# A gated recurrence on one core: GpSimd's wait moved to half A's hh transpose, the x transpose in quarters, and five memsets on VectorE

## The chip, the cores and the metric

The kernel runs on one core of a Trainium2 chip. The metric is the device time of one execution in microseconds; where several runs are shown it is their median. The engines are called PE (TensorE's matmuls; PEld is its weight load), DVE (VectorE), ACT (ScalarE), POOL (GpSimd) and SP (SyncE, which issues the DMAs).

## The reference, cut to what matters

For a batch of 8, 512 time steps and 512 features, a recurrence runs over the steps, and its states are added to the input. In the kernel's shorthand r is the first half of the fused gates, z the second, and hh is `h @ wh_W + wh_b`.

```python
def step(h, x_t):
    fused = sigmoid(concatenate([x_t, h], -1) @ w_W + w_b)
    hidden_state, output_state = split(fused, 2, -1)       # r, z
    memory_state = x_t @ wx_W + wx_b + hidden_state * (h @ wh_W + wh_b)
    h_new = output_state * h + (1.0 - output_state) * tanh(memory_state)
    return h_new, h_new
_, hs = scan(step, h0, swapaxes(x, 0, 1))
return x + swapaxes(hs, 0, 1)
```

All is float32.

## The kernel before, in words

**Tiling.** The 512 units of the state lie as 128 partitions by 4 chunks. Chunks 0 and 1 are half A, chunks 2 and 3 half B. For each half the state is kept in a ring of eight buffers (hT, lines 97 to 101; NH = 8). A buffer has 32 columns, of which the 8 of the batch for this step's place s in its group of four steps are filled, and the others stay zero. So a matmul whose stationary operand is such a buffer adds to the 8 rows of its own step only. Four steps (GS = 4) make a group g, and s is the place in it.

**PSUM.** There are two sets of banks, one for each parity of the group: A holds hh, z and r of half A (192 columns), Z holds z of half B (64), B holds r and hh of half B (128). Two further banks, xp, gather x times its weights for a whole group: `prefill` (line 154) issues sixteen matmuls of 384 columns a group, four in each step. `seed` (line 150, ScalarE) puts the bias into xp first, `spread` (line 166, ScalarE) copies the gates' parts from xp into the next group's banks A, B and Z, and `turn_x` (line 171, VectorE) transposes the 128 columns X, which are x @ wx_W, into the tile md1.

**The step.** The loop at line 194 is unrolled 512 times, under a schedule written out by hand, so every engine gets its instructions in the order of the text. PE runs ORDER (line 20): A0 B0 A1 with half A's new state as weights, A2 A3 with half B's, then the rest of B, then Z, then four xp matmuls of the group after the next. VectorE's order is in lines 284 to 295. Per half there are three transposes of PSUM (r and z by `turned` at L223, hh by `turn_h` at L235), the scan `memory` (L252: hh times r plus x), the product `kept` (L263: z times h) and the scan `update` (L275: the new state into the ring). ScalarE (act, L145) does the sigmoids of r, z and minus z, and tanh. After the two halves come, by s, spread A (s = 0), spread B and Z (s = 1), turn_x of the next group (s = 2), or seed of the group g + 3 (s = 3), which writes the bank that turn_x of the next group has read. Last, GpSimd adds state and input into the output tile (L308), one instruction a half. Every 16 steps SP loads 256 KB of x and stores 256 KB of output.

**The wait for GpSimd.** `update` of step i overwrites the ring buffer that GpSimd read seven steps earlier. The wait for that is not put on update but on `kept`, ahead of it on VectorE, and only once there is such an addition, from i = 8 on:

```python
inst = nc.vector.tensor_tensor(
    hd1[hf][i % 2][:, :, :, 1], ...
).ins
if i + 1 - NH in pool_done:
    tc.add_manual_dep(inst, pool_done[i + 1 - NH][hf].name, SYNC)
```

An instruction that waits for two semaphores has a wait instruction ahead of it (EVENT_SEMAPHORE in the trace, on the same line). Such instructions lie on the queue of the engine, but don't count as busy.

Of the kernel before, what the change touches and what calls it, by code (L numbers as in the profile page):

```python
# [13 lines left out]
NQ = 4  # L14
GS = 4
B = 8
HU = 64
SYNC = mybir.DependencyInfo(mybir.DependencyClass.Sync, mybir.DependencyReason.DATA)

ORDER = "A0 B0 A1 A2 A3 B1 B2 B3 Z0 Z1 Z2 Z3"  # L20
# [3 lines left out]
XP = {"A": slice(0, 192), "Z": slice(192, 256), "X": slice(256, 384), "B": slice(384, 512)}  # L24
# [3 lines left out]
def tile_cond_rnn_residual(  # L28
# [31 lines left out]
    nc = tc.nc  # L60
# [12 lines left out]
    def load_x(c):  # L73
        if c < NCH:
            t_ = xin_p.tile([P, NQ, TC * B], F32, tag="xin", name=f"xin_{c}")
            nc.sync.dma_start(out=t_, in_=x[c].rearrange("p (k n) -> p k n", k=NQ))
            xins[c] = t_
# [14 lines left out]
    for k in range(NQ):  # L92
# [4 lines left out]
    NH = 2 * GS  # L97
    hT = [
        [const.tile([P, 32, 2, 2], F32, name=f"hT{n}{i}") for i in range(NH)]
        for n in "AB"  # L100
    ]

    md0 = [[const.tile([P, 32, 2, 2], F32, name=f"md0{n}{i}") for i in range(2)] for n in "AB"]
    md1 = [const.tile([P, 2, 32, 2, 2], F32, name=f"md1{i}") for i in range(2)]
    hd0 = [[const.tile([P, B, 2, 2], F32, name=f"hd0{n}{i}") for i in range(2)] for n in "AB"]
    hd1 = [[const.tile([P, B, 2, 2], F32, name=f"hd1{n}{i}") for i in range(2)] for n in "AB"]
    zs = [[const.tile([P, 2, B], F32, name=f"z{n}{i}") for i in range(2)] for n in "AB"]
    zeros = const.tile([P, 32], F32, name="zeros")
    for t_ in [zeros] + hT[0] + hT[1] + hd0[0] + hd0[1] + md0[0] + md0[1]:
        nc.gpsimd.memset(t_, 0.0)  # L110

    def state(hf, i):

        s = i % GS
        return hT[hf][i % NH][:, B * s : B * s + B, :, 1]
# [12 lines left out]
    xps = [psum.tile([P, 512], F32, name=f"xp{q}") for q in range(2)]  # L128

    def mm(out_, lhsT, rhs, start=False):  # L130
        nc.tensor.matmul(  # L131
            out_, lhsT, rhs, start=start, stop=False, skip_group_check=True
        )
# [10 lines left out]
    def act(key, *args, **kw):  # L144
        inst = nc.scalar.activation(*args, **kw).ins  # L145
        if key in written:
            tc.declare_no_dep(inst, written[key], reason="ordered through VectorE")
        written[key] = inst

    def seed(g):  # L150

        nc.scalar.copy(xps[g % 2], bias)

    def prefill(g):

        c, t0 = divmod(g * GS, TC)
        for k in range(NQ):
            for j in range(NQ):
                mm(
                    xps[g % 2][32 * j : 32 * j + 32, 64:448],  # L160
                    xins[c][:, k, t0 * B : t0 * B + 32],
                    wx[:, k, j, :],
                )
            yield

    def spread(g, names):

        for n in names:
            nc.scalar.copy(banks[g % 2][n], xps[g % 2][:, XP[n]])

    def turn_x(g):
        nc.vector.transpose(
            md1[g % 2][:, :, :, :, 1].rearrange("p h n c -> p h c n"), xps[g % 2][:, XP["X"]]
        )

    def take(it, n=None):
        while n is None or n > 0:
            if next(it, it) is it:
                return
            n = None if n is None else n - 1  # L180
# [3 lines left out]
    for g in range(2):  # L184
        seed(g)
        take(prefill(g))
        if g == 0:
            spread(0, "ABZ")
            turn_x(0)
            seed(0)  # L190
    ctx.enter_context(tc.manual_schedule())

    pool_done = {}
    for i in range(T):
        g, s = divmod(i, GS)
        c, t = divmod(i, TC)
        ps = banks[g % 2]
        if t == 0:
            load_x(c + 3)
            ot = out_p.tile([P, NQ, TC, B], F32, tag="ot", name=f"ot_{c}")  # L200
        if s == 0:
            pre = prefill(g + 2) if g + 2 < NG else iter(())

        for n in ORDER.split():
            bank, k = n[0], int(n[1])
            hs = hT[k // 2][i % NH][:, :, k % 2, 1]
            for j in range(NQ):
                mm(ps[bank][32 * j : 32 * j + 32, :], hs, wh[:, k, j, WH[bank]])
        take(pre, 1)

        rows = slice(B * s, B * s + B)
        def flat(t_):
            return t_.rearrange("p n c s -> p (n c s)")

        raw = {
            "h": (ps["A"][:, :HU], ps["B"][:, HU:]),
            "z": (ps["A"][:, HU : 2 * HU], ps["Z"]),
            "r": (ps["A"][:, 2 * HU :], ps["B"][:, :HU]),
        }

        def turned(n, hf):
            t_ = work.tile([P, 2, 32], F32, tag=f"t{n}{hf}", name=f"t{n}{hf}_{i}")
            nc.vector.transpose(t_.rearrange("p c n -> p (c n)"), raw[n][hf])  # L223
            return t_[:, :, rows]

        def turn_r(hf):
            act(
                ("r", hf, g % 2, s),
                md0[hf][g % 2][:, rows, :, 1].rearrange("p n c -> p c n"),
                turned("r", hf),  # L230
                AF.Sigmoid,
            )

        def turn_h(hf):
            nc.vector.transpose(  # L235
                md1[g % 2][:, hf, :, :, 0].rearrange("p n c -> p c n"), raw["h"][hf]
            )

        def turn_z(hf):
            tz = turned("z", hf)  # L240
            act(("z", hf, i % 2), zs[hf][i % 2], tz, AF.Sigmoid)
            act(
                ("zc", hf, i % 2),
                hd0[hf][i % 2][:, :, :, 1].rearrange("p n c -> p c n"),
                tz,
                AF.Sigmoid,
                scale=-1.0,
            )

        def memory(hf):  # L250
            m = work.tile([P, B, 2, 2], F32, tag=f"m{hf}", name=f"m{hf}_{i}")
            nc.vector.tensor_tensor_scan(  # L252
                flat(m),
                flat(md0[hf][g % 2][:, rows]),
                flat(md1[g % 2][:, hf, rows]),
                0.0,
                ALU.mult,
                ALU.add,
            )
            act(("n", hf, i % 2), hd1[hf][i % 2][:, :, :, 0], m[:, :, :, 1], AF.Tanh)  # L260

        def kept(hf):
            inst = nc.vector.tensor_tensor(  # L263
                hd1[hf][i % 2][:, :, :, 1],
                zs[hf][i % 2].rearrange("p c n -> p n c"),
                state(hf, i),
                ALU.mult,
            ).ins

            if i + 1 - NH in pool_done:  # L270
                tc.add_manual_dep(inst, pool_done[i + 1 - NH][hf].name, SYNC)

        def update(hf):
            s1 = (i + 1) % GS
            nc.vector.tensor_tensor_scan(  # L275
                flat(hT[hf][(i + 1) % NH][:, B * s1 : B * s1 + B]),
                flat(hd0[hf][i % 2]),
                flat(hd1[hf][i % 2]),
                0.0,
                ALU.mult,  # L280
                ALU.add,
            )

        turn_r(0)
        turn_h(0)
        turn_z(0)
        memory(0)
        turn_h(1)
        kept(0)
        turn_r(1)  # L290
        update(0)
        turn_z(1)
        memory(1)
        kept(1)
        update(1)

        if g + 1 < NG:
            if s == 0:
                spread(g + 1, "A")
            elif s == 1:  # L300
                spread(g + 1, "BZ")
            elif s == 2:
                turn_x(g + 1)
            elif s == 3 and g + 3 < NG:
                seed(g + 3)
        done = []
        for hf in range(2):
            inst = nc.gpsimd.tensor_tensor(  # L308
                ot[:, 2 * hf : 2 * hf + 2, t, :].rearrange("p c n -> p n c"),
                xins[c][:, 2 * hf : 2 * hf + 2, t * B : t * B + B].rearrange("p c n -> p n c"),  # L310
                state(hf, i + 1),
                ALU.add,
            ).ins
            done.append(inst)
        pool_done[i + 1] = done
        if t == TC - 1:
            nc.sync.dma_start(out=out[c], in_=ot.rearrange("p k t b -> p (k t b)"))
            xins.pop(c)
# [62 lines left out]
```

## Time and profile before

| what | value |
|---|---|
| time, median of 3 runs | 1774.58 us (1774.36 to 1774.95) |
| the profiled execution's own time | 1775.63 us |
| its span (first to last instruction) | 1773.9 us |
| granted TensorE clock, mean | 0.998 |
| VectorE, instructions in the trace, waits included | 8826, of which 6274 compute |
| HBM traffic | 14.96 MB read, 8.39 MB written |
| GpSimd, L308 | 125.8 us for half A's 512 additions, 124.3 us for half B's |

The profile is one execution. In the groups and timelines a row has the line of the kernel, the engine, the operation, output and inputs by their names (buffer numbers left out), the shape and a count. Timelines begin with the start and the duration in us; idle time of the engine before an instruction and what ended it stand in brackets. VectorE's rows overlap a little[...]. In the answers on waits, a row has who waited for whom, the us in total, the times, and the longest. Transfers of instructions show in the profile as DMA queues of their own: 416 packets with 6.82 MB in one, and 116 packets with 0.94 MB in another.

### The profile page before, as it was taken

The page shows a single profiled execution, that of the slowest core. Times are in us where ns is not written, and L with a number is a line of the kernel's source. Part 1 is how long each engine was busy: PE and PEld are TensorE (multiplying, and loading weights), DVE is VectorE, ACT ScalarE, POOL GpSimd, SP SyncE. Part 2 cuts the span into 40 slices and gives each one's busy share as a digit, 9 for nine tenths or more (in the row PEclk, how much of TensorE's full clock was granted, in tenths as well). Part 3 has the DMA queues.
Part 4 walks back from the last instruction along what each step waited for, and adds up shares of the span by engine and source line. Part 5 has one row for each costly group of instructions (what it writes and reads, how often), then busy time and mean ns, then how long its engine had stood idle before and what let it go on. Part 6 is the DMA issues. An engine that isn't in the chain of part 4 may idle for free.

```text
span 1773.9 us, 121405 instructions
## 1 busy us (share of the span) xinstructions
PE 1751.6 (99%) x53312; PEld 1422.4 (80%) x53312; DVE 1129.7 (64%) x6274; ACT 857.4 (48%) x4610; POOL 253.4 (14%) x1053
## 2 busy tenths in 40 slices
PE   7999999999999999999999999999999999999998
PEld 5888888888888888888888888888888888888887
DVE  2666666666666666666666666666666666666665
ACT  2444444444454444444444444444444444444444
POOL 1111111111111111111111111111111111111111
PEclk9999999999999999999999999999999999999999
DMA  4000000000000000000000000000000000000000
GB/s 174 16 4 16 16 16 16 6 15 16 17 16 16 4 16 17 16 16 5 16 16 16 16 15 5 16 16 16 17 4 16 16 16 16 4 16 11 10 10 10
DMA packets 11236, 31.11 MB, mean 18 GB/s; under 512 B 1361, under 2 KB 1361, under 8 KB 10705
## 3 DMA queue, kind: packets, MB, share of 16 engines
q1 hardware_dynamic: 10704, 23.35, 3.9%
q8 instruction: 416, 6.82, 1.6%
q14 instruction: 116, 0.94, 0.2%
HBM read 14.96 MB, written 8.39 MB: 13 GB/s over the span
## 4 chain that ended last, share of the span: by engine, by line
PE 95%; DVE 2%; DMA 1%; ACT 1%; issue 1%; SPq 0%; POOLq 0%; DVEq 0%; POOL 0%; ACTq 0%
PE A L131 40%; PE B L131 24%; PE xp L131 18%; PE Z L131 13%; DMA hin<-in_h_dram 1%; DVE tr L223 1%; DVE hTA L275 0%; ACT md0A L145 0%; DVE m L252 0%; DVE hd1A L263 0%; DMA wx<-in_wx_dram 0%; DVE hTB L275 0%; ACT zB L145 0%; DVE tz L223 0%; DVE md L235 0%
## 5 line engine op out<-in xcount | busy, mean ns | idle before, releaser
L131 PE MATMUL A<-wh,hTA 128*32 128x192 f32 x8192 | 527.1, 327 | 11.2 <-DVE hTB L120 7.4
L145 ACT ACTIVATE md0A<-tr 128x16 f32<-128x16 f32 x512 | 120.9, 236 | 723.6 <-DVE tr L223 723.6
L131 PE MATMUL A<-wh,hTB 128*32 128x192 f32 x8192 | 455.5, 340 | 2.1 <-DVE hTB L275 1.5
L131 PEld LDWEIGHTS A<-wh,hTA 128*32 128x32 f32 x8192 | 275.8, 137 | 220.7 <-DVE hTA L275 212.5
L223 DVE STREAM_TRANSPOSE tr<-A 128x64 f32<-128x64 f32 x512 | 127.9, 250 | 479.9 <-PE A L131 479.9
L131 PE MATMUL xp<-wx,xin 128*32 128x384 f32 x4096 | 425.9, 486 | 0.0
L131 PE MATMUL B<-wh,hTA 128*32 128x128 f32 x8192 | 414.8, 273 | 0.0
L131 PEld LDWEIGHTS A<-wh,hTB 128*32 128x32 f32 x8192 | 273.2, 142 | 105.3 <-DVE hTB L275 98.9
L131 PEld LDWEIGHTS B<-wh,hTA 128*32 128x32 f32 x8192 | 325.2, 136 | 10.3
L131 PE MATMUL B<-wh,hTB 128*32 128x128 f32 x8192 | 318.3, 273 | 0.0
L308 POOL TENSOR_TENSOR ot<-xin,hTA 128x16 f32<-128x16 f32 x512 | 125.8, 246 | 1127.2 <-DVE hTA L275 1038.0
L131 PEld LDWEIGHTS B<-wh,hTB 128*32 128x32 f32 x8192 | 248.3, 136 | 0.0
L131 PE MATMUL Z<-wh,hTB 128*32 128x64 f32 x8192 | 222.6, 225 | 0.0
L131 PE MATMUL Z<-wh,hTA 128*32 128x64 f32 x8192 | 217.2, 223 | 0.0
L131 PEld LDWEIGHTS Z<-wh,hTA 128*32 128x32 f32 x8192 | 200.9, 141 | 0.0
L131 PEld LDWEIGHTS Z<-wh,hTB 128*32 128x32 f32 x8192 | 182.1, 147 | 0.0
L308 POOL TENSOR_TENSOR ot<-xin,hTB 128x16 f32<-128x16 f32 x512 | 124.3, 243 | 389.6 <-DVE hTB L275 389.6
L145 ACT ACTIVATE md0B<-tr 128x16 f32<-128x16 f32 x512 | 119.2, 233 | 108.0 <-DVE tr L223 106.6
L275 DVE TENSOR_TENSOR_SCAN hTB<-hd0B,hd1B 128x32 f32<-128x32 f32 x512 | 115.1, 225 | 55.0 <-DVE hd1B L263 1.0
L235 DVE STREAM_TRANSPOSE md<-B 128x64 f32<-128x64 f32 x512 | 146.7, 286 | 0.6 <-issue 0.5
L235 DVE STREAM_TRANSPOSE md<-A 128x64 f32<-128x64 f32 x512 | 135.8, 265 | 0.0
L252 DVE TENSOR_TENSOR_SCAN m<-md0B,md 128x32 f32<-128x32 f32 x512 | 133.8, 261 | 0.5
(42 smaller groups left out, 1767.3 us busy)
## 6 DMA issues: line engine op xcount, KB each, us to landing
xin<-in_x_dram SPq DMA_DIRECT2D x32, 256.0 KB, 3.0
out_dram<-ot SPq DMA_DIRECT2D x32, 256.0 KB, 2.1
wx<-in_wx_dram SPq DMA_DIRECT2D x4, 768.0 KB, 6.6
wh<-in_wh_dram SPq DMA_DIRECT2D x4, 768.0 KB, 13.5
bias<-in_bias_dram SPq DMA_DIRECT2D x4, 64.0 KB, 2.0
hin<-in_h_dram SPq DMA_DIRECT2D x1, 16.0 KB, 15.0
```

The source lines that it names most:

```text
L131: nc.tensor.matmul(out_, lhsT, rhs, start=start, stop=False, skip_group_check=True)
L145: inst = nc.scalar.activation(*args, **kw).ins
L223: nc.vector.transpose(t_.rearrange("p c n -> p (c n)"), raw[n][hf])
L235: nc.vector.transpose(md1[g % 2][:, hf, :, :, 0].rearrange("p n c -> p c n"), raw["h"][hf])
L252: nc.vector.tensor_tensor_scan(flat(m), flat(md0[hf][g % 2][:, rows]), flat(md1[g % 2][:, hf, rows]), 0.0, ALU.mult, ALU.add,)
L275: nc.vector.tensor_tensor_scan(flat(hT[hf][(i + 1) % NH][:, B * s1 : B * s1 + B]), flat(hd0[hf][i % 2]), flat(hd1[hf][i % 2]), 0.0, ALU.mu ...
L308: inst = nc.gpsimd.tensor_tensor(ot[:, 2 * hf : 2 * hf + 2, t, :].rearrange("p c n -> p n c"), xins[c][:, 2 * hf : 2 * hf + 2, t * B : t * ...
```

## The change

There are three edits. The wait for GpSimd moves from the two `kept` to `turn_h(0)`, and there it is for the later of the two additions of its step. `turn_x` transposes 32 columns instead of 128 and is issued in every step, with the quarter e = s, ahead of spread and seed; for the first group all four quarters are issued at the start. And of the memsets at the start, the first five of the tiles hd0 and md0 (`DVE_FILL`) go to VectorE. With this, VectorE has 16 instructions in each step, wait instructions included.

```diff
--- before.py
+++ after.py
@@ -15,6 +15,9 @@
 GS = 4
 B = 8
 HU = 64
+
+
+DVE_FILL = 5
 SYNC = mybir.DependencyInfo(mybir.DependencyClass.Sync, mybir.DependencyReason.DATA)
 
 ORDER = "A0 B0 A1 A2 A3 B1 B2 B3 Z0 Z1 Z2 Z3"
@@ -106,8 +109,10 @@
     hd1 = [[const.tile([P, B, 2, 2], F32, name=f"hd1{n}{i}") for i in range(2)] for n in "AB"]
     zs = [[const.tile([P, 2, B], F32, name=f"z{n}{i}") for i in range(2)] for n in "AB"]
     zeros = const.tile([P, 32], F32, name="zeros")
-    for t_ in [zeros] + hT[0] + hT[1] + hd0[0] + hd0[1] + md0[0] + md0[1]:
+    for t_ in [zeros] + hT[0] + hT[1]:
         nc.gpsimd.memset(t_, 0.0)
+    for n, t_ in enumerate(hd0[0] + hd0[1] + md0[0] + md0[1]):
+        (nc.vector if n < DVE_FILL else nc.gpsimd).memset(t_, 0.0)
 
     def state(hf, i):
 
@@ -168,9 +173,11 @@
         for n in names:
             nc.scalar.copy(banks[g % 2][n], xps[g % 2][:, XP[n]])
 
-    def turn_x(g):
+    def turn_x(g, e):
+
+        c0 = XP["X"].start + 32 * e
         nc.vector.transpose(
-            md1[g % 2][:, :, :, :, 1].rearrange("p h n c -> p h c n"), xps[g % 2][:, XP["X"]]
+            md1[g % 2][:, e // 2, :, e % 2, 1], xps[g % 2][:, c0 : c0 + 32]
         )
 
     def take(it, n=None):
@@ -186,7 +193,8 @@
         take(prefill(g))
         if g == 0:
             spread(0, "ABZ")
-            turn_x(0)
+            for e in range(NQ):
+                turn_x(0, e)
             seed(0)
     ctx.enter_context(tc.manual_schedule())
 
@@ -232,9 +240,12 @@
             )
 
         def turn_h(hf):
-            nc.vector.transpose(
+            inst = nc.vector.transpose(
                 md1[g % 2][:, hf, :, :, 0].rearrange("p n c -> p c n"), raw["h"][hf]
-            )
+            ).ins
+
+            if hf == 0 and i + 1 - NH in pool_done:
+                tc.add_manual_dep(inst, pool_done[i + 1 - NH].name, SYNC)
 
         def turn_z(hf):
             tz = turned("z", hf)
@@ -260,15 +271,12 @@
             act(("n", hf, i % 2), hd1[hf][i % 2][:, :, :, 0], m[:, :, :, 1], AF.Tanh)
 
         def kept(hf):
-            inst = nc.vector.tensor_tensor(
+            nc.vector.tensor_tensor(
                 hd1[hf][i % 2][:, :, :, 1],
                 zs[hf][i % 2].rearrange("p c n -> p n c"),
                 state(hf, i),
                 ALU.mult,
-            ).ins
-
-            if i + 1 - NH in pool_done:
-                tc.add_manual_dep(inst, pool_done[i + 1 - NH][hf].name, SYNC)
+            )
 
         def update(hf):
             s1 = (i + 1) % GS
@@ -295,24 +303,20 @@
         update(1)
 
         if g + 1 < NG:
+            turn_x(g + 1, s)
             if s == 0:
                 spread(g + 1, "A")
             elif s == 1:
                 spread(g + 1, "BZ")
-            elif s == 2:
-                turn_x(g + 1)
             elif s == 3 and g + 3 < NG:
                 seed(g + 3)
-        done = []
         for hf in range(2):
-            inst = nc.gpsimd.tensor_tensor(
+            pool_done[i + 1] = nc.gpsimd.tensor_tensor(
                 ot[:, 2 * hf : 2 * hf + 2, t, :].rearrange("p c n -> p n c"),
                 xins[c][:, 2 * hf : 2 * hf + 2, t * B : t * B + B].rearrange("p c n -> p n c"),
                 state(hf, i + 1),
                 ALU.add,
             ).ins
-            done.append(inst)
-        pool_done[i + 1] = done
         if t == TC - 1:
             nc.sync.dma_start(out=out[c], in_=ot.rearrange("p k t b -> p (k t b)"))
             xins.pop(c)
```

## The prediction

> **What bounds the kernel now.** I read the page first, then the waits, then the timeline of single steps. The page says that TensorE is never idle:
>
> ```profile
> PE 1751.6 (99%) x53312; PEld 1422.4 (80%) x53312; DVE 1129.7 (64%) x6274; ACT 857.4 (48%) x4610; POOL 253.4 (14%) x1053
> PE 95%; DVE 2%; DMA 1%; ACT 1%; issue 1%; SPq 0%; POOLq 0%; DVEq 0%; POOL 0%; ACTq 0%
> ```
>
> Matmul ends are modelled, so 99% does not show that PE has no slack. The waits show where its weight loads stand still:
>
> ```profile
> PEld A L131 <- DVE hTA L275: 212.5, 509, 1.5
> PEld A L131 <- DVE hTB L275: 98.9, 499, 0.6
> ```
>
> The first is harmless in an ordinary step: the load of hTA waits while the xp matmuls still run (xp to the next A matmul is 0.645 us in the median, also where the load waits less). The second is not. Two timelines around a load of hTB:
>
> ```profile
> 53.37 0.54 PE L131 MATMUL A<-wh,hTA 128*32 128x192 f32 x8
> ...
> 53.62 0.59 PEld L131 LDWEIGHTS A<-wh,hTB 128*32 128x32 f32 x16
> ...
> 53.69 0.87 PE L131 MATMUL A<-wh,hTB 128*32 128x192 f32 x16
> ...
> 54.34 0.43 PE L131 MATMUL B<-wh,hTA 128*32 128x128 f32 x8
> ...
> 56.67 0.54 PE L131 MATMUL A<-wh,hTA 128*32 128x192 f32 x8
> ...
> 57.03 0.54 PEld L131 LDWEIGHTS A<-wh,hTB 128*32 128x32 f32 x16 [0.17 <-DVE hTB L275]
> 57.03 0.89 PE L131 MATMUL A<-wh,hTB 128*32 128x192 f32 x16
> ...
> 57.74 0.40 PE L131 MATMUL B<-wh,hTA 128*32 128x128 f32 x8
> ```
>
> Count steps from 0. In step 7 (the upper four lines) hTB was loaded 0.25 us after the A1 matmuls began, and A1 to B took 0.97 us (0.325 + 0.650 in the trace's ns). In step 8 it was loaded at 0.36, and the same stretch took 1.07. All other PE stretches are the same in all steps within some ns. So PE alone needs 3.307 us a step (325 + 218 + 325 + 650 + 219 + 436 + 239 + 250 + 645 ns), and the median step takes 3.381: the loop A matmuls, VectorE and ScalarE, hTB, A matmuls is the longer one, by 0.074 us.
>
> **Why hTB is late: the wait for GpSimd.** kept (L263) waits for ScalarE (z) and for GpSimd. Two semaphores make one extra wait instruction each:
>
> ```profile
> L263 DVEq EVENT_SEMAPHORE  x1008: 21/21/21, 55.4 to 1769.9; - x168
> ```
>
> 1008 is 2 x 504: steps 8 to 511. The first eight steps have no earlier GpSimd addition to wait for, so they are the kernel without that wait. Step 5 and a late step:
>
> ```profile
> 44.61 0.25 DVE L223 STREAM_TRANSPOSE tr<-A 128x64 f32<-128x64 f32 x1 [1.09 <-PE A L131]
> ...
> 45.71 0.22 DVE L275 TENSOR_TENSOR_SCAN hTA<-hd0A,hd1A 128x32 f32<-128x32 f32 x1
> ...
> 46.64 0.22 DVE L275 TENSOR_TENSOR_SCAN hTB<-hd0B,hd1B 128x32 f32<-128x32 f32 x1
> ```
>
> ```profile
> 807.30 0.25 DVE L223 STREAM_TRANSPOSE tr<-A 128x64 f32<-128x64 f32 x1 [1.01 <-PE A L131]
> ...
> 808.44 0.23 DVE L275 TENSOR_TENSOR_SCAN hTA<-hd0A,hd1A 128x32 f32<-128x32 f32 x1
> ...
> 809.44 0.23 DVE L275 TENSOR_TENSOR_SCAN hTB<-hd0B,hd1B 128x32 f32<-128x32 f32 x1
> ```
>
> From the step's first transpose to hTB: 2.03 us without the wait, 2.14 with it. Each wait instruction takes the queue 0.065 us (start to start), and the two add up to 0.11.
>
> **Block crossings.** One median step in eleven is longer by 0.17 to 0.37 us. Number VectorE's records in the trace, waits included, from 0: record 63 and each 128th after it come late. An example is record 3903:
>
> ```profile
> 798.32 0.27 DVE L252 TENSOR_TENSOR_SCAN m<-md0B,md 128x32 f32<-128x32 f32 x1
> 799.03 0.18 DVE L263 TENSOR_TENSOR hd1B<-zB,hTB 128x16 f32<-128x16 f32 x1 [0.45 <-ACT hd1B L145]
> ```
>
> ScalarE's hd1B, named there, does not feed this product; it lies 0.71 us behind m instead of 0.36. There are 69 such records. By position in a step of 17 (18 with turn_x), the step grows by: positions 0 to 3 (tr, md, tz, wait) nothing; 4 to 11 (m to tz of Z) 0.17 to 0.37; 12 and 13 nothing; 14 to 16 (hd1B, wait, hTB) 0.17 to 0.37; 17 (turn_x) nothing. A step of 17.25 records on average moves through all of them: 45 of the 69 cost, together 12.35 us.
>
> **The change, part by part.** *Wait moved.* Both kept lose the second semaphore and so their wait instruction. turn_h(0) (L235) had no wait at all, and takes GpSimd's as its only one. What it waits for, the addition of seven steps ago, ended some 23 us earlier. Behind it on VectorE are tz, m and all of the half; behind those ScalarE and PE. A satisfied wait inside an instruction has near rows: md<-B waits for PE and starts 0.14 us after m. Bounds: nothing, or 0.065 if it became an instruction of its own; below nothing is excluded, since a wait takes nothing away. I take nothing. Then tr to hTB is 2.03, hTB to the load 0.279, load to the next tr 0.955 to 0.977 while PE itself waits: 3.27 to 3.29 us, now below PE's 3.307. PE becomes the bound, and the load falls 0.254 us after A1, where step 7 (0.252) lost nothing; that step is 3.309 long. I take 3.308. From 0.31 on loss is seen (0.042 in steps 1 to 6), so the margin is small; 10 ns lost in every step would be 5 us.
>
> The Trainium skill, "Perfetto Trace Analysis", section "Identifying the Most-Contended Engine", says to read TensorE's headroom from LDWEIGHTS busy, not matmul busy. That is 80% here, hence some 350 us of room; the row of step 7 leaves 496 x 0.073 = 36. The measured step decides.
>
> *turn_x in quarters.* One transpose of 128 columns (0.404 us, L172) in one step of four becomes one of 32 columns in every step. A 64-column one takes 0.21 to 0.29, so I estimate 0.15 to 0.2. It starts after hTB and lies in VectorE's idle time before the next tr (0.69 us remain where the whole one runs now, 1.01 elsewhere): nothing. With no cover it would cost 512 x 0.2 = 102 us less 128 x 0.4 = 51. The quarters in steps s = 0 and 1 read the bank while ScalarE copies from it; no row shows that overlap, but a slower quarter still has 0.7 us to spare. The last quarter is in s = 3, and seed(g+3), which overwrites the bank, must wait for it: seed starts not 0.13 us after ScalarE's hd1B but some 0.65 later (hTB 0.27 after hd1B, quarter 0.14 behind hTB, 0.2 long, 0.04 to be seen). It takes 0.58 and ends 1.2 us after hd1B; queued behind it is md0A of the next step, which starts 1.8 after hd1B. Cost nothing, 0.6 us to spare. PE's xp matmuls, which need the seed, come later still.
>
> *Fill.* Five memsets go from GpSimd to VectorE (0.12 to 0.2 us each on GpSimd). VectorE has nothing until 14.9 us, and the start waits for hin's landing at 22.5. No cost.
>
> *16 records a step.* 13 instructions (12 and a quarter) and 3 waits (L252, both L275). 128 is 8 x 16, so crossings stay at one place. Which? Before step 0 VectorE has 7 records now; 5 memsets and 3 more transposes make 15. 15 + 3 x 16 = 63: the late record is the tr<-A of step 3 and of every eighth step after it, position 0, which costs nothing today (4 of 4), because it waits for PE anyway. Bounds: nothing, or, were I several records off, 62 x 0.35 = 22 us. I take nothing, since one record earlier and three later are harmless too.
>
> A rule against this: the skill's "Runtime: NRT & Kernel Launch", "Instruction fetch mechanics", has blocks of 256 instructions, and a crossing "mostly hidden". Then alignment is worth nothing, and the result is 1725.1 + 12.3 = 1737.4. The rows show every 128th record and 12.35 us, so I keep these.
>
> **The sum**, against the span (before to after, us): until the first tr 26.17, same; step 0 4.70, same; steps 1 to 6 20.44 to 20.11 (one crossing); step 7 3.31, same; steps 8 to 503 1689.78 to 496 x 3.308 + 0.69 = 1641.46 (0.69 is a stall of PE's own at 1448.9 us, which I leave in); steps 504 to 510, without xp matmuls and so bound by the loop, 23.66 to 7 x 3.28 = 22.96; the rest 5.80 to 5.69. 1773.86 becomes 1724.40, 49.5 less: 36 from the step, 12.3 from crossings, the rest from the end. The profiled execution took 1775.63, 1.73 over its span, and the median of runs is 1.05 below it: 1774.58 - 49.5 = 1725.1.
>
> **Rivals.** (1) As summed, 1722 to 1729: 0.82. (2) GpSimd's wait costs its 0.065 in turn_h as an instruction: the loop is then 3.33 to 3.35, and 17 records let crossings wander again. Saved is 496 x 0.04 + 1 = 21, so 1754. For it: the wait is now early in the longer half; against: turn_h has no other semaphore. 0.04. (3) The crossings lie at a costly place, 62 x 0.2 to 0.35: 1737 to 1747. Against: my count of 15. 0.06. Or the load of hTB is late by some ns and 1729 to 1737 comes out: 0.04. (4) Slower: seed. ScalarE runs in order, so a late seed holds up md0A of the next step, in each of 127 groups. It decides from 0.6 us of extra delay on, and from 0.6 + 49.5/127 = 0.99 the whole change is lost. If seed were tied to the next step's md<-A (its tr starts 1.55 after hd1B; 0.17 + 0.27 + 0.04 more), it would end at 2.61, 0.78 behind md0A's place at 1.83: 127 x 0.78 = 99 less 49.5 gives 1824. For it: this is the only new wait between engines; against: the quarter is done half a step before that. 0.03. That the saving is used up just about to nothing: 0.01.
>
> A difference under 0.2% (3.5 us) cannot be told from none. Faster 0.96, same 0.01, slower 0.03. The range reaches into (3): 1721 to 1738.
>
> **What would show it.** Right: no EVENT_SEMAPHORE at kept's line, 1536 in the loop in all; tr to hTB 2.03; A1 to B 0.975 and steps of 3.31; PEld's wait for hTB nearly gone; no step over 3.4 but the PE stall. Wrong: tr to hTB at 2.08 or more (2), long steps every eighth (3), md0A waiting for seed (4), or hTB's load over 0.26 us behind A1.

## The result, and the profile after

The changed kernel takes 1726.88 us in the median of 4 runs (1726.29 to 1727.97), the kernel before 1774.76 beside it. The ratio is 0.9731, with a 95% interval of 0.9719 to 0.9743: 47.9 us less, where 49.5 had been forecast. The profiled execution took 1726.31 us; its span is 1724.5 (forecast: 1724.4).

The answers that correspond to those shown of before follow; line numbers have moved (kept is L274, the update L283, hh's transpose L243). First the page's busy times and chain:

```profile
PE 1706.2 (99%) x53312; PEld 1489.8 (86%) x53312; DVE 1138.6 (66%) x6663; ACT 894.8 (52%) x4610; POOL 252.9 (15%) x1048
PE 98%; DMA 1%; DVE 0%; issue 0%; SPq 0%; ACT 0%; POOLq 0%; POOL 0%; DVEq 0%
```

PE's busy share is 99% as before, although the time fell by 2.7%. It could not tell the two apart; the chain (95% to 98% PE) does so a little. The groups say more. In a group, the last part is the idle time before it and what ended it:

```profile
L136 PEld LDWEIGHTS A<-wh,hTB 128*32 128x32 f32 x8192 | 302.4, 137 | 33.0 <-DVE hTB L283 1.2 <-issue 0.2
```

The idle time before the weight load for hTB fell from 105.3 us to 33.0, and the part of it that the view puts down to hTB from 98.9 to 1.2. It names nothing for most of the 33.0, so this is not the whole wait; PE's rows of one step show what is left of it:

```profile
809.22 0.55 PE L136 MATMUL A<-wh,hTA 128*32 128x192 f32 x8
...
809.47 0.59 PEld L136 LDWEIGHTS A<-wh,hTB 128*32 128x32 f32 x16
...
810.19 0.44 PE L136 MATMUL B<-wh,hTA 128*32 128x128 f32 x8
```

The load begins 0.25 us after the A1 matmuls, as in step 7 of the trace before. From A1 to B it takes 0.97 us; the median of steps 8 to 503 is 0.975, where it was 1.053 before and 0.975 had been forecast.

Kept has lost its wait instructions: the answer for its line holds the two products and no EVENT_SEMAPHORE.

```profile
L274 DVE TENSOR_TENSOR hd1A<-zA,hTA x512: 142/154/186, 27.0 to 1719.7; 128x16 f32<-128x16 f32 x171
L274 DVE TENSOR_TENSOR hd1B<-zB,hTB x512: 175/177/187, 27.9 to 1720.6; 128x16 f32<-128x16 f32 x171
```

One step's timeline, VectorE:

```profile
807.15 0.25 DVE L231 STREAM_TRANSPOSE tr<-A 128x64 f32<-128x64 f32 x1 [0.90 <-PE A L136]
...
808.27 0.23 DVE L283 TENSOR_TENSOR_SCAN hTA<-hd0A,hd1A 128x32 f32<-128x32 f32 x1
...
809.19 0.23 DVE L283 TENSOR_TENSOR_SCAN hTB<-hd0B,hd1B 128x32 f32<-128x32 f32 x1
809.33 0.22 DVE L179 STREAM_TRANSPOSE md<-xp 128x32 f32<-128x32 f32 x1
810.47 0.25 DVE L231 STREAM_TRANSPOSE tr<-A 128x64 f32<-128x64 f32 x1 [0.92 <-PE A L136]
```

From the first transpose to hTB it takes 2.04 us (2.14 before), and the step 3.32 (the median of all is 3.307, 3.381 before). The quarter of x lies behind hTB, and 0.92 us of idle time follow it.

By stretches, from the first transposes of the steps in both traces (us):

| stretch | before | forecast | after |
|---|---|---|---|
| start to the first transpose | 26.17 | 26.17 | 26.08 |
| step 0 | 4.70 | 4.70 | 3.51 |
| steps 1 to 6 | 20.44 | 20.11 | 20.13 |
| step 7 | 3.31 | 3.31 | 3.30 |
| steps 8 to 503 | 1689.78 | 1641.46 | 1642.95 |
| steps 504 to 510 | 23.66 | 22.96 | 22.89 |
| the rest | 5.80 | 5.69 | 5.69 |

All 64 of VectorE's late records now are the step's first transpose, and no step is longer for them. Seven long steps remain among steps 8 to 503: 353, 369, 385 and so on to 449, together 2.2 us. They are PE's own: no late record of VectorE falls into them.

### The profile page after: what moved, and what is told of

The parts are those of the page before. It is cut to its first block, busy times and chain, and to the rows that moved or that the text cites. A ratio compares the mean times of both kernels' runs of the same rounds, so it can differ in the third digit from the quotient of the medians.

```text
span 1724.5 us, 121032 instructions
## 1 busy us (share of the span) xinstructions
PE 1706.2 (99%) x53312; PEld 1489.8 (86%) x53312; DVE 1138.6 (66%) x6663; ACT 894.8 (52%) x4610; POOL 252.9 (15%) x1048
## 4 chain that ended last, share of the span: by engine, by line
PE 98%; DMA 1%; DVE 0%; issue 0%; SPq 0%; ACT 0%; POOLq 0%; POOL 0%; DVEq 0%
PE A L136 39%; PE B L136 25%; PE xp L136 19%; PE Z L136 14%; DMA hin<-in_h_dram 1%; DMA wx<-in_wx_dram 0%; DVE tr L231 0%; ACT md0A L150 0%; DVE hTA L283 0%; DVE m L263 0%; SPq L85 0%; DVE md L243 0%; SPq L79 0%; POOLq L379 0%; POOL ot L314 0%
## 5 line engine op out<-in xcount | busy, mean ns | idle before, releaser
L136 PE MATMUL A<-wh,hTA 128*32 128x192 f32 x8192 | 555.6, 327 | 9.5 <-DVE hTB L125 7.3
L136 PEld LDWEIGHTS A<-wh,hTA 128*32 128x32 f32 x8192 | 321.3, 137 | 184.6 <-DVE hTA L283 176.2
L136 PE MATMUL B<-wh,hTA 128*32 128x128 f32 x8192 | 450.9, 273 | 0.0
L136 PE MATMUL xp<-wx,xin 128*32 128x384 f32 x4096 | 444.2, 486 | 0.0
L136 PEld LDWEIGHTS B<-wh,hTA 128*32 128x32 f32 x8192 | 364.7, 136 | 1.6
L136 PE MATMUL B<-wh,hTB 128*32 128x128 f32 x8192 | 336.4, 273 | 0.0
L136 PEld LDWEIGHTS A<-wh,hTB 128*32 128x32 f32 x8192 | 302.4, 137 | 33.0 <-DVE hTB L283 1.2
L136 PEld LDWEIGHTS B<-wh,hTB 128*32 128x32 f32 x8192 | 266.6, 137 | 0.0
L136 PE MATMUL Z<-wh,hTB 128*32 128x64 f32 x8192 | 240.6, 226 | 0.0
L136 PEld LDWEIGHTS Z<-wh,hTB 128*32 128x32 f32 x8192 | 200.1, 148 | 0.0
L283 DVE TENSOR_TENSOR_SCAN hTB<-hd0B,hd1B 128x32 f32<-128x32 f32 x512 | 115.2, 225 | 52.7
L243 DVE STREAM_TRANSPOSE md<-B 128x64 f32<-128x64 f32 x512 | 146.9, 287 | 0.0
L243 DVE STREAM_TRANSPOSE md<-A 128x64 f32<-128x64 f32 x512 | 139.0, 271 | 0.0
```

Of the source, the lines that this page charges most:

```text
L136: nc.tensor.matmul(out_, lhsT, rhs, start=start, stop=False, skip_group_check=True)
L243: inst = nc.vector.transpose(md1[g % 2][:, hf, :, :, 0].rearrange("p n c -> p c n"), raw["h"][hf]).ins
L283: nc.vector.tensor_tensor_scan(flat(hT[hf][(i + 1) % NH][:, B * s1 : B * s1 + B]), flat(hd0[hf][i % 2]), flat(hd1[hf][i % 2]), 0.0, ALU.mu ...
```

## The experiments

Two theories stood against each other at first. Mine: two savings. GpSimd's wait lengthened the loop, and block crossings lengthened single steps. The rival: one of the two does it all.

**wait_only** is the kernel before with the wait moved and nothing else.

```diff
@@ kept @@
...
-            if i + 1 - NH in pool_done:
-                tc.add_manual_dep(inst, pool_done[i + 1 - NH][hf].name, SYNC)
@@ turn_h @@
...
+            if hf == 0 and i + 1 - NH in pool_done:
+                tc.add_manual_dep(inst, pool_done[i + 1 - NH][1].name, SYNC)
```

> The kernel before with one edit: GpSimd's wait moved from both kept to turn_h(0); x still turned whole in s = 2, all memsets on GpSimd. Theory (two savings that add up: the wait shortens the loop below PE's 3.307 us, and 16 records a step keep block crossings in idle time): ordinary steps of 3.307 us, but crossings still wander through the step (15.25 records on average, 61 crossings); summed from their prices in the trace before they cost 10 to 11 us. 1774.8 - 36.5 - 1.5 + 1 = about 1738. Rival A, the alignment does nearly all and the wait was hidden: about 1774. Rival B, the wait does all and the crossings don't matter once PE is the bound: about 1727.

Measured: 1732.78 us, ratio 0.9769 (0.9755 to 0.9784). The ordinary step is 3.307, as said. 24 steps are longer for a crossing, by 6.2 us together, where I had expected 10 to 11; five stalls of PE's take 1.2. So neither rival is right, though the second comes nearer, and neither is my price for a crossing. Sorted by the instruction that comes late, before / here, in us: m 0.30 / 0.31, md<-B 0.22 / 0.22, half A's kept 0.35 / 0.11, tr<-B 0.24 / 0.00, hTA 0.36 / 0.32, tz<-Z 0.27 / 0.24, half B's kept 0.35 / 0.00, hTB 0.36 / 0.32. What became cheap is what stood close behind kept's wait instructions, which are gone. The 0.03 to 0.04 less at hTA, tz and hTB is about the room that the loop now has below PE (0.039, by no_xp below).

**wait_back** is the changed kernel with the wait put back on both kept, for the addition of the same half, as before.

```diff
@@ turn_h @@
...
-            if hf == 0 and i + 1 - NH in pool_done:
-                tc.add_manual_dep(inst, pool_done[i + 1 - NH].name, SYNC)
@@ kept @@
...
+            if i + 1 - NH in pool_done:
+                tc.add_manual_dep(inst, pool_done[i + 1 - NH][hf].name, SYNC)
```

> The changed kernel with GpSimd's wait put back on both kept: quarters of x and the fill stay, 18 records a step. Theory: ordinary steps of 3.381 us again, 72 wandering crossings for 13.8 us, the start 1.2 us shorter as in the changed kernel: about 1775, as before. Rival A (quarters and fill save something by themselves): 1762 or less. Rival B (the wait cost nothing): about 1739, from crossings alone.

Measured: 1774.11 us, ratio 1.0002 (0.9993 to 1.0012). Ordinary steps of 3.378, long steps for 14.1 us. The quarters and the fill save nothing without the wait's move; with 18 records a step the crossings wander as before.

**fill7** puts two more memsets on VectorE, and so two more records ahead of the loop.

```diff
-DVE_FILL = 5
+DVE_FILL = 7
```

> The changed kernel with seven memsets on VectorE in place of five, nothing else. By the count of records the late one moves from the step's first transpose to the update of half B, in one step of eight. Theory: every eighth step is 0.33 to 0.36 us longer, 64 x 0.33 = 21 us: about 1748. Rival (crossings are hidden now that PE is the bound, or the place isn't what the count says): 1727, or long steps elsewhere.

Measured: 1744.68 us, ratio 0.9836 (0.9821 to 0.9851), 17.8 above the changed kernel. In its trace every eighth step is 0.30 to 0.35 us longer, and the late record is hTB each time; in steps 8 to 503 this makes 19.7 us. It ends below the 1748 expected, since 0.32 is the low end of my price and PE's stalls take 0.8 us in place of 2.2. VectorE's timeline around such a step:

```profile
811.39 0.28 DVE L263 TENSOR_TENSOR_SCAN m<-md0B,md 128x32 f32<-128x32 f32 x1
811.71 0.18 DVE L274 TENSOR_TENSOR hd1B<-zB,hTB 128x16 f32<-128x16 f32 x1
812.34 0.22 DVE L283 TENSOR_TENSOR_SCAN hTB<-hd0B,hd1B 128x32 f32<-128x32 f32 x1 [0.45 <-ACT hd1B L150]
812.48 0.21 DVE L179 STREAM_TRANSPOSE md<-xp 128x32 f32<-128x32 f32 x1
```

hTB is 0.63 us behind the product, where it is 0.28 in other steps. The profile puts this down to ScalarE's hd1B; but the steps between have the same hd1B and no such gap. The place of the late record was moved by two more records ahead of the loop, and by nothing else.

**no_xp** leaves out the xp matmuls in the loop, that is, the share of x from the third group on.

```diff
-        take(pre, 1)
```

> The changed kernel without the xp matmuls in the loop (the share of x is left out from group 2 on, so 0.645 us of PE's work in each step is gone). Theory (PE is the bound of the changed kernel, with the loop through VectorE just under it): steps shrink only to that loop, 3.27 us as in the last seven steps, and PE's own stalls vanish: 1727 - 19 - 2 = about 1706. Rival (the loop still sets the time, PE merely looks full): 1727, no change. Rival (the loop is far shorter than PE): down towards 1727 - 330.

Measured: 1704.24 us, ratio 0.9609 (0.9593 to 0.9625). The step is 3.268, and no step of the loop is long. PE's timeline shows that it now has to wait (a matmul of the program has two rows in the trace, so x16 are eight):

```profile
801.54 0.43 PE L136 MATMUL Z<-wh,hTB 128*32 128x64 f32 x16
802.28 0.56 PE L136 MATMUL A<-wh,hTA 128*32 128x192 f32 x8 [0.31 <-DVE hTA L282]
```

Taking 0.645 us from PE shortens the step by 0.039: PE is the bound of the changed kernel, and the loop through VectorE is right below it.

**wait_first** moves GpSimd's wait to the step's first transpose, which waits for PE as well.

```diff
@@ turn_h @@
-            if hf == 0 and i + 1 - NH in pool_done:
-                tc.add_manual_dep(inst, pool_done[i + 1 - NH].name, SYNC)
@@ turned @@
+            if n == "r" and hf == 0 and i + 1 - NH in pool_done:
+                tc.add_manual_dep(inst, pool_done[i + 1 - NH].name, SYNC)
```

> The changed kernel with GpSimd's wait on the step's first transpose, which waits for PE already, in place of turn_h(0): one wait instruction more, 17 records. Theory if that instruction holds the later of the two waits: 0.065 us more in the loop, steps of 3.33 to 3.35, and 68 wandering crossings for 10 us: 1748 to 1758. If it holds GpSimd's wait and runs in VectorE's idle time: steps of 3.307 and the crossings alone, about 1737. No difference at all (1727) would speak against both the count of records and the price of a wait instruction.

Measured: 1751.19 us, ratio 0.9867 (0.9854 to 0.9881). The step is 3.336, with a wait instruction in 504 steps (the answer for the transposes' line):

```profile
L231 DVEq EVENT_SEMAPHORE  x504: 21/21/21, 53.7 to 1744.0; - x168
```

From the transpose to hTB it takes 2.03 us, 2.04 in the changed kernel. So the 0.029 that a step is longer lie between PE's last A matmul and the transpose: the wait instruction is paid there although GpSimd's addition had ended 24 us before. In the trace's records the wait instruction holds PE's semaphore and the transpose GpSimd's; so it begins only when PE is done, and stands in the loop. (At kept, in the kernel before, it held ScalarE's.) Its 0.065 less the room between the loop (3.268 in no_xp) and PE (3.307) is 0.026. With 17 records the crossings wander again, and 35 of the 68 cost some 8.5 us. And md<-A and tz behind it, free to cross in the kernel before, now cost 0.25 and 0.13 us: the price of a crossing goes with the wait instruction just ahead of it.

The next runs are about what the table leaves: step 0 and PE's seven long steps. The changed kernel was run once more beside them.

> The changed kernel once more, beside the next three: 1726 to 1728.

Measured: 1726.95 us (1726.55 to 1727.36). Its profile differs from the first where the chip is free to: step 0 takes 4.00 us (3.51 in the first), and five PE stalls cost 2.4.

**fill4** has four memsets on VectorE, all of hd0, and none of md0.

```diff
-DVE_FILL = 5
+DVE_FILL = 4
```

> The changed kernel with four memsets on VectorE in place of five: md0's first tile is filled by GpSimd again. Theory (the start got 1.2 us shorter since ScalarE's first sigmoid waits for VectorE alone, and so the load of its table runs ahead of the wait): the table is loaded after the wait again, step 0 takes 4.70 us in place of 3.51, 1.2 us more: about 1728. The crossing moves to the second transpose, free by its price before. Rival (the shorter step 0 comes from something else): no change.

Measured: 1726.68 us (1726.53 to 1727.64), ratio 0.9733: no difference from after_again, where 1.2 us more had been expected. Yet the trace shows what was expected of it. All 64 late records are the second transpose, and none costs. ScalarE's timeline at the start:

```profile
26.51 1.28 ACT L150 ACT_TABLE_LOAD   x1 [9.67 <-DVE tr L231]
27.81 0.23 ACT L150 ACTIVATE md0A<-tr 128x16 f32<-128x16 f32 x1
```

and that of the changed kernel:

```profile
16.80 1.28 ACT L150 ACT_TABLE_LOAD   x1
26.36 0.24 ACT L150 ACTIVATE md0A<-tr 128x16 f32<-128x16 f32 x1 [8.27 <-DVE tr L231]
```

Step 0 is 4.70 us again. It is 4.70 in the kernel before and in wait_only too, where the load also comes at 26.2 to 26.5 us; in the nine other traces the load comes at 16.7 to 16.9, and step 0 takes 3.38 to 4.43. So the fifth memset did free the table's load, but how much is gained depends on something else: PE is granted half its clock from about 19 us on, and the full clock again at 26.1 us in the first profile of the changed kernel, at 27.2 in after_again, at 28.5 in load_mid; step 0 takes 3.51, 4.00 and 4.43. In fill4's own profile the clock came back at 28.8, where by these figures only an estimated 0.3 us (4.70 less 4.43) would have been to gain. Against PE's stalls, 1.1 to 2.4 us from profile to profile (1.1 in fill4's), the rest can't be measured.

**load_mid** was to move x's load from the chunk's first step to its ninth, away from the output's store.

```diff
-            load_x(c + 3)
...
+        if t == TC // 2:
+            load_x(c + 3)
```

> The changed kernel with the 256 KB load of x issued in the ninth step of each 16 in place of the first, where it follows the 256 KB store of the output. Theory (the seven long steps 353, 369 to 449 are PE waiting for a block of its instructions, whose transfer is behind these 512 KB): they vanish, 2.2 us less: about 1724.7. Rival (the load alone does it): they move to the tenth step of 16, no change of the time. Rival (another cause): they stay.

Measured: 1726.95 us (1725.54 to 1727.37), and the stalls stay, six of them. The edit tested nothing. SyncE's queue in its trace:

```profile
1404.57 0.34 SPq L322 DMA_DIRECT2D out_dram<-ot  x1
1405.01 0.38 SPq L79 DMA_DIRECT2D xin<-in_x_dram  x1
```

The load follows the store at once, as in the changed kernel, since nothing on SyncE's queue makes it wait. **load_mid2** ties it to an addition of GpSimd; **store_mid** holds the store back in the same way and leaves the load at the start of the chunk. Their edits in this order:

```diff
-            load_x(c + 3)
...
+        if t == TC // 2:
+            load_x(c + 3, pool_done[i])
...
+            if after is not None:
+                tc.add_manual_dep(inst, after.name, SYNC)
```

```diff
+        if t == TC // 2 and c:
+            inst = nc.sync.dma_start(out=out[c - 1], in_=ot_was.rearrange("p k t b -> p (k t b)")).ins
+            tc.add_manual_dep(inst, pool_done[i].name, SYNC)
...
-            nc.sync.dma_start(out=out[c], in_=ot.rearrange("p k t b -> p (k t b)"))
```

The output's last store stays at the end in store_mid.

> The changed kernel with the load of x tied to GpSimd's addition of the eighth step of its 16, so that it really starts half a chunk after the output's store (in the run before it, only its place in the program moved, and it started where it always had). Theory (PE's block of instructions comes late behind store and load together): the long steps at places 0 and 1 of 16 vanish, and the load alone makes none at place 8 or 9: 1.5 to 2 us less, 1725. Rival (the load alone does it): they move to place 8 or 9, same time. Rival (the store alone): they stay at place 1, same time.

> The changed kernel with the output's store held back until GpSimd's addition of the eighth step of the next 16, while the load of x stays at the chunk's start. Theory (store and load together): no long steps, 1725. Rival (the load alone): they stay at place 1 of 16. Rival (the store alone): they move to place 8 or 9.

Measured: load_mid2 1724.93 us (1724.13 to 1725.22), ratio 0.9720 (0.9707 to 0.9733); store_mid 1724.80 us (1724.30 to 1725.08), ratio 0.9719 (0.9706 to 0.9732). In load_mid2's trace load and store are 26 us apart:

```profile
1401.96 0.34 SPq L324 DMA_DIRECT2D out_dram<-ot  x1
1428.45 0.33 SPq L79 DMA_DIRECT2D xin<-in_x_dram  x1
```

Neither trace has a single long step after step 7. So PE's stalls hang on store and load together (512 KB), and neither transfer alone makes them. In the changed kernel's weight loads the stall looks like this:

```profile
1407.81 0.17 PEld L136 LDWEIGHTS xp<-wx,xin 128*32 128x32 f32 x4
1408.61 0.11 PEld L136 LDWEIGHTS xp<-wx,xin 128*32 128x32 f32 x2 [0.63 <-issue]
```

The profile names nothing in the program that it waits for. PE's blocks of instructions (416 packets of 16 KB; in no_xp, with 8095 fewer records of PE, 385) come every 4 us or so; the last one ahead of this stall started 5.7 us after the one before it, while store and load (issued at 1403.0 and 1403.4) were on the DMA engines. That fits a block held up by the transfers, but the trace doesn't show which block PE waited for. Nor is it known why few of the chunks have a stall: in all traces they lie in the second step of a chunk, and only in steps 305 to 449. Both versions beat the changed kernel by some 2 us; their runs don't overlap with those of it, though the ratios' intervals do.

## Why the prediction was right

**The loop and the wait.** Shown. The first eight steps of the trace before were a fair copy of the changed VectorE queue: 2.03 us to hTB was read there, 2.04 is measured; the step was to be 3.308, and the steps 8 to 503 less their stalls have a mean of 3.308. The loop without PE's bound was summed to 3.27 to 3.29, and no_xp has 3.268. But only step 7 was a copy of the whole step. Steps 1 to 6 take 3.35 us in both kernels, since PE's load of hTB begins 0.34 us behind hTB there, and 0.28 from step 7 on. In those steps the trace has a wait instruction ahead of this load, and the load holds GpSimd's semaphore: it is the first use of a ring buffer that GpSimd's memset filled. The prediction saw the late load, not this cause. GpSimd's wait costs nothing on hh's transpose. On the first transpose it costs a wait instruction (wait_first), so the place matters: here it is free on an instruction that has no other semaphore.

**PE is next.** Shown by no_xp. The floor of 3.307 from one step (step 7) held for 496. LDWEIGHTS busy, by which (beside the share of peak FLOPs) the Trainium skill's "Perfetto Trace Analysis", "Identifying the Most-Contended Engine", judges headroom, is now 86%; by it 14% would still be free. The runs decide against it here: no_xp shows that PE's work sets the changed kernel's step.

**Crossings.** The total was right, the way it was split was not. That 16 records a step bring each late record to the first transpose was counted from the trace before, and all 64 lie there; fill7 moved them to hTB by the same count. But the 12.35 us are the crossings' price in the loop as it was. In the kernel with the wait moved and nothing aligned they cost 6.2. So the wait's move alone brings 41 of some 48 us (1773.6 to 1732.8), and alignment on top of it about 6, where my sum had 36 and 12.3. (Between wait_only and the changed kernel step 0 also gets 1.2 us shorter, and PE's stalls take 1.0 more; these two nearly cancel.) "Two savings that add up" holds for their sum only, since the move takes part of the crossings' cost with it. It comes out, since the changed kernel has neither the longer loop nor a crossing that costs. The skill's "Runtime: NRT & Kernel Launch", "Instruction fetch mechanics", which calls crossings mostly hidden, would have given 1737.4, 10.5 us too high for the changed kernel; and fill7, with the same 16 records at another place, shows 20 us at stake.

**Seed and spread.** The last quarter's effect on seed was foreseen in size: ScalarE waits 0.51 us for it (64.3 us in 126 waits). That both spreads would wait too was not: I had them read the bank beside VectorE, but they stand behind the quarters in the program, and wait for them:

```profile
ACT A L174 <- DVE md L179: 66.0, 127, 0.8
ACT xp L157 <- DVE md L179: 64.3, 126, 0.8
ACT B L174 <- DVE md L179: 57.2, 127, 0.5
```

It costs nothing: md0A, queued behind them, still waits for its transpose each time. The quarter takes 0.218 us; the estimate was 0.15 to 0.2.

**Two terms were mis-sized, and cancel.** "Step 0 4.70, same" and "Fill. No cost": step 0 took 3.51, 1.2 less, since the memset of md0's first tile on VectorE leaves ScalarE's first sigmoid with one semaphore, and its table is loaded ahead of the wait. And PE's stalls, left at 0.69, cost 2.2. Together they add 0.3 us to the forecast, the small terms take 0.2 off, and the span came out 0.1 over it. That it came so close is luck.

**The last 1.8 us** between 1725.1 and 1726.88 are not in the span: the median of the runs before lay 1.05 below its profiled execution, that of the changed kernel 0.57 above. The stalls and the clock at the start, which differ from run to run, would be enough for that; which of them it is was not settled.

## What to carry to other kernels

The first turns of a loop can run without a wait that later turns have, and are then a cheap estimate of what removing that wait brings. They can also have waits of their own, as steps 1 to 6 do here; look for a turn that is free of both (step 7), which gives the next bound. When an instruction on the critical loop has two semaphores, give one of them to a neighbour ahead of it on the same queue that has none. When an in-order queue shows late instructions at a fixed count, count the records of a turn: a turn that divides the block keeps all crossings at one place, and a few fillers choose the place.

## What the runs showed of the hardware that was not expected

- VectorE's crossings cost by what stands ahead of them. In the kernel before, wait_only and wait_first, the first instruction behind a wait instruction pays 0.29 to 0.37 us, the second 0.17 to 0.28, the third 0 to 0.21, later ones at most 0.07; those before or behind which VectorE idles anyway (the first transpose, x's) pay nothing. That VectorE's sequencer is held at the wait instruction, and so comes late to the block's end, would explain it; this was not tested.
- PE stalls in some chunks, by up to 0.78 us, when a store and a load of 256 KB each are moved at once (4 to 7 stalls in the profiles of the changed kernel, fill4 and load_mid), and not when they are 26 us apart (none in load_mid2 and store_mid).
- The full clock came back to PE between 25.3 and 28.8 us after the start, from profile to profile. Where the table was loaded early, step 0 was the longer the later the clock came back: 3.51 us with 26.1, 4.43 with 28.5.
